# Score columns of two attention layers become rows on all partitions: by DMA through a DRAM scratch row instead of by transposes on TensorE

## The chip, the cores and the metric

The kernel runs on one core of one Trainium2 chip. The metric is the device time of one execution in microseconds (us); the time before is the median of three runs. The profile is one further execution, taken by the hardware profiler. Its engines are PE (TensorE, matmuls), PEld (TensorE weight loads, which overlap PE), DVE (VectorE), ACT (ScalarE), POOL (GpSimd) and SP (SyncE, which in this kernel only issues DMAs).

## The reference

Input is a batch of 64 graphs with 256 nodes and 256 features each (`x`, 64 x 256 x 256, float32), and an adjacency matrix per graph (`adj`, 64 x 256 x 256, int32). Four layers follow, each with a layer norm and a relu in front and a residual around it:

- layer 0: masked self attention with 8 heads
- layer 1: graph attention with one head
- layer 2: three rounds of messages `A^T (h W)` into a GRU cell
- layer 3: graph attention with 4 heads

What the change concerns are the scores of layers 1 and 3, cut to their core:

```python
# layer 1
f1 = Wh @ a1; f2 = Wh @ a2
e = leaky_relu(f1[:, :, None] + f2[:, None, :], 0.2)
attention = softmax(where(mask > 0, e, -9e15), axis=1)
out = elu(attention @ Wh)
# layer 3, per head h
s_src = einsum('bnhc,hc->bnh', f, a_src); s_dst = einsum('bnhc,hc->bnh', f, a_dst)
logits = leaky_relu(s_src[:, :, None, :] + s_dst[:, None, :, :], 0.2)
probs = softmax(where(adj == 1, logits, -9e15), axis=2)
```

A score matrix is the sum of a column (one number per row node) and a row (one number per column node). On the chip nodes lie on partitions. The column is then one number per partition, which an activation adds as its bias for nothing. The row has to lie on every one of the 128 partitions, and this is what both kernels have to make from a column.

## The kernel before, in words

Two graphs are one "pair" (512 nodes, T = 4 tiles of 128 nodes), and there are 32 pairs. A short preparation loads and combines weights. After it the kernel describes every step of every pair as a task: an engine, an estimated duration, and the buffers that it reads and writes (`add`, line 59). `Plan.order` (line 96) then takes tasks greedily by their earliest start in its own model of time, over all pairs, and so writes one fixed order of instructions per engine. It does this for 18 settings (how many `w4` buffers stay spare for the oldest pair, and how finely start times are compared), and `Plan.best` (line 179) keeps the setting whose order comes out shortest in a model with jitter. Matmuls of layer 2 come last among PE tasks that can start at the same moment, so they fill PE while other layers wait for DVE and ACT. On the chip every engine runs its list in order; waits between engines and DMAs are semaphores. A DMA task counts as 0.7 us on SP plus a latency (3.5 us for an adjacency, 3.0 us for `x`).

Buffers are counted by `SLOTS` (line 237): 28 work buffers `w4` of 4 KB per partition, 2 `adj` of 4 KB, 8 banks of PSUM (`ps`), 4 `w2` of 2 KB, 4 of `x`, and small ones. A buffer is taken when its first task is ordered, and comes free after its last.

The steps around the change:

- `load_adj` (530) loads a pair's adjacency once per layer, after the layer norm's statistics. The mask tasks (551, 687, 971) turn it into additive bf16 masks; layer 2 (790) turns it into a float matrix `am` in a `w4` buffer of its own.
- Layer 1 (683): four products give `Wh` and the two score columns; line 701 copies the columns to `f12`. The task `spread` (707) turns each of four columns into a row on all partitions by a transpose of the column broadcast to 128 x 128 (`row_to_all`, line 679; the trace shows its line 681). The row lies in a PSUM bank `psf`. Four Prelu activations (716) read it with the other column as bias. Eight bf16 transposes bring the mask (728), and mask add, max, exp and the product (760) follow.
- Layer 3 (968): four products (978), copied by DVE with a bias (982) into `f`. For each of 4 heads `spread` (989) makes a row of 512 numbers by four transposes (line 681 too), and an eviction (line 444 on ACT or 445 on DVE) takes it to a `w4` buffer of `sd`. Then for each tile of 128 nodes come four Prelu (1006), mask add (1012), max (1017), four exp (542), eight transposes (1029) with evictions, and per graph a product (1050), transposes back (1065), a scaling (1072) and the residual (1077).

Of the kernel before, what the change touches and what calls it, by code (L numbers as in the profile page):

```python
# [11 lines left out]
FP = mybir.dt.float32  # L12
BF = mybir.dt.bfloat16
I32 = mybir.dt.int32
AF = mybir.ActivationFunctionType
ALU = mybir.AluOpType
AX = mybir.AxisListType

P = 128
# [19 lines left out]
class Plan:  # L39
# [19 lines left out]
    def add(self, forms, reads=(), writes=(), latency=0.0, claims=()):  # L59

        t = Task()
        t.pair, t.forms = len(self.pairs) - 1, [forms] if isinstance(forms, tuple) else forms
        t.before, t.after, t.bufs, t.latency = set(), [], [], latency
        t.end = t.engine = None
        t.order, t.layer = len(self.pairs[-1]), self.layer  # L70
        for items, writing in ((reads, False), (writes, True)):
            for item in items:
                buf, part = item if isinstance(item, tuple) else (item, None)
                if buf not in t.bufs:
                    t.bufs.append(buf)
                keys = [part] if part is not None else list(buf.parts) + [None]
                for key in keys:
                    last, readers = buf.parts.setdefault(key, [None, []])
                    whole = buf.parts.get(None, [None, []])
                    for x in (last, whole[0]):  # L80
                        if x is not None:
                            t.before.add(x)
                    if writing:
                        t.before.update(readers)
                        t.before.update(whole[1])
                for key in keys:
                    if writing:
                        buf.parts[key] = [t, []]
                    else:
                        buf.parts[key][1].append(t)  # L90
        t.before.discard(t)
        t.bufs += [b for b in claims if b not in t.bufs]
        self.pairs[-1].append(t)
        return t
# [101 lines left out]
def tile_adj_preln_d4(  # L196
# [33 lines left out]
    T = 4  # L230
# [5 lines left out]

    SLOTS = {
        "x": (4, [P, T * D], FP, 0),
        "adj": (2, [P, T * N], I32, 1),
        "w4": (28, [P, T * D], FP, 9),  # L240
        "f3": (2, [P, T, E3], FP, 0),
        "mask": (4, [P, T * N], BF, 1),
        "ps": (8, [P, 512], FP, 2),
# [5 lines left out]
        "zs": (6, [P, H0], FP, 2),  # L249
        "rz": (6, [P, H0], FP, 2),  # L250
        "f12": (2, [P, T, 2], FP, 0),
    }
    psum = ctx.enter_context(tc.tile_pool(name="psum", bufs=1, space=bass.MemoryType.PSUM))
    tiles = {"ps": [psum.tile([P, 512], FP, name=f"ps_{i}") for i in range(SLOTS["ps"][0])]}
# [151 lines left out]


    work = ctx.enter_context(tc.tile_pool(name="work", bufs=1))
    for tag, (n, shape, dtype, _) in SLOTS.items():
        if tag not in tiles:  # L410
            tiles[tag] = [work.tile(shape, dtype, name=f"{tag}_{i}") for i in range(n)]
    plan = Plan({tag: v[0] for tag, v in SLOTS.items()}, {tag: v[3] for tag, v in SLOTS.items()})

    def buf(tag):
        return Buf(tag, tiles[tag])

    def w4():
        return buf("w4")

    def bank():  # L420
        return buf("ps")
# [4 lines left out]
    def dve2(n):  # L426
        return 0.065 + n / 1920.0
# [7 lines left out]
    def tok(ap, d=D):  # L435
        return ap.rearrange("p (t d) -> p t d", d=d)
# [91 lines left out]
                mm(ps()[:, c * D : (c + 1) * D], chunk(src, k, 2 * g + c), rhs[:, k, :], start=k == 0, stop=k == 1)  # L528

    def load_adj(p, mv):  # L530
        at = buf("adj")
        add(
            (SP, 0.7, lambda: nc.sync.dma_start(tok(at(), N), adj[2 * p : 2 * p + 2].rearrange("g (c p) d -> p (g c) d", p=P))),
            reads=[mv], writes=[at], latency=3.5,
        )
        return at
# [11 lines left out]
    def layer0(xt, p):  # L548
        at, hT = norm_relu_T(xt, p)
        mb = buf("mask")  # L550
        add((V, dve2(T * N), lambda: nc.vector.tensor_scalar(mb(), at(), 0.0, MASKED, ALU.is_le, ALU.mult), True), reads=[at, hT], writes=[mb])
        for g in range(2):
            add(
                (G, pool(2 * D), lambda g=g: nc.gpsimd.tensor_add(
# [121 lines left out]
        half = lambda: xt()[:, g * N2 : (g + 1) * N2]  # L676
        add((V, dve(N2), lambda: nc.vector.tensor_add(half(), ps(), half())), reads=[ps], writes=[(xt, g)])

    def row_to_all(ps, col):

        nc.tensor.transpose(ps, col.to_broadcast([P, P]), ident)  # L681

    def layer1(xt, p):
        at, hT = norm_relu_T(xt, p)
        m1 = buf("mask")
        add(
            (V, dve2(T * N), lambda: nc.vector.tensor_scalar(
                m1(), at(), 0.0, MASKED, ALU.is_le, ALU.mult), True),
            reads=[at, hT], writes=[m1],
        )  # L690
        wh, f12 = w4(), buf("f12")
        for t in range(T):
# [9 lines left out]
                reads=[ps], writes=[(f12, t)],  # L702
            )
            add((A, act(D), lambda t=t, ps=ps: nc.scalar.copy(tok(wh())[:, t, :], ps()[:, 0:D])), reads=[ps], writes=[(wh, t)])
        psf = bank()

        def spread():
            for t in range(T):
                row_to_all(psf()[:, t * P : (t + 1) * P], f12()[:, t, 0:1])

        e = w4()
        add((PE, 4 * TURN, spread), reads=[f12], writes=[psf], claims=[e])
        for t in range(T):
            g = t // 2
            add(
                (A, act(N, 1), lambda t=t, g=g: nc.scalar.activation(
                    tok(e(), N)[:, t, :], psf()[:, g * N : (g + 1) * N], AF.Prelu,
                    bias=f12()[:, t, 1:2], alpha=ALPHA)),
                reads=[psf, f12], writes=[(e, t)],
            )  # L720
        psb = bank()
        psm = lambda: psb().bitcast(BF).rearrange("p (t n) -> p t n", n=N)
# [63 lines left out]

    def layer2(xt, p):
        at, hT, h = norm_relu_T(xt, p, tokens=True)
        am = w4()
        add((V, dve2(T * N), lambda: nc.vector.tensor_scalar(am(), at(), 0.0, None, ALU.not_equal), True), reads=[at, hT], writes=[am])  # L790
        at_o = lambda b, o: tok(b(), N2)[:, o, :]

        def messages(h):
# [174 lines left out]
    def layer3(xt, p):  # L968
        at, hT = norm_relu_T(xt, p)
        mb = buf("mask")  # L970
        add((V, dve2(T * N), lambda: nc.vector.tensor_scalar(mb(), at(), 1.0, MASKED, ALU.not_equal, ALU.mult), True), reads=[at, hT], writes=[mb])
        f = buf("f3")
        for t in range(T):
            ps = bank()
# [8 lines left out]
                reads=[ps], writes=[(f, t)],  # L983
            )
        sd = [w4() for i in range(2)]
        for h in range(H3):
            ps = bank()

            def spread(h=h, ps=ps):
                for t in range(T):  # L990
                    row_to_all(ps()[:, t * P : (t + 1) * P], f()[:, t, D + H3 + h : D + H3 + h + 1])

            add((PE, 4 * TURN, spread), reads=[f], writes=[ps], claims=[sd[h // 2]])
            add(
                evict(N2, lambda h=h: tok(sd[h // 2](), N2)[:, h % 2, :], ps),
                reads=[ps], writes=[(sd[h // 2], h % 2)],
            )
        for g in range(2):
            zs, rz = buf("zs"), buf("rz")
            eT = [w4() for k in range(2)]  # L1000
            for ti in range(2):
                t = 2 * g + ti
                e, mx = w4(), buf("mx")
                for h in range(H3):
                    add(
                        (A, act(N, 1), lambda t=t, g=g, h=h, e=e: nc.scalar.activation(
                            tok(e(), N)[:, h, :], tok(sd[h // 2](), N2)[:, h % 2, g * N : (g + 1) * N], AF.Prelu,
                            bias=f()[:, t, D + h : D + h + 1], alpha=ALPHA)),
                        reads=[(sd[h // 2], h % 2), (f, t)], writes=[(e, h)],
                    )  # L1010
                add(
                    (V, dve(T * N), lambda t=t, e=e: nc.vector.tensor_tensor(
                        tok(e(), N), tok(e(), N), tok(mb(), N)[:, t : t + 1, :].to_broadcast([P, H3, N]), ALU.add), True),
                    reads=[mb], writes=[e],
                )
                add(
                    (V, dve(T * N), lambda e=e, mx=mx: nc.vector.tensor_reduce(
                        mx()[:, 0:H3], tok(e(), N), AX.X, ALU.max, negate=True)),
                    reads=[e], writes=[mx],
                )  # L1020
                rows = [(i, i, H3 * ti + i) for i in range(H3)]
                add(exp_group(e, mx, zs, rows, f"3_{p}_{t}"), reads=[mx], writes=[e, (zs, ti)])
                for k in range(2):
                    ps = bank()

                    def turn(k=k, ps=ps, e=e):
                        for i in range(2):
                            for c in range(2):
                                nc.tensor.transpose(  # L1029
                                    tok(ps(), P)[:, 2 * i + c, :], tok(e(), N)[:, 2 * k + i, c * P : (c + 1) * P], ident  # L1030
                                )

                    add((PE, 4 * TURN, turn), reads=[e], writes=[ps], claims=[eT[k]])
                    add(
                        evict(
                            N2,
                            lambda dst=eT[k], ti=ti: tok(dst(), N)[:, :, ti * P : (ti + 1) * P],
                            lambda ps=ps: tok(ps(), P),
                        ),
                        reads=[ps], writes=[(eT[k], ti)],  # L1040
                    )
# [90 lines left out]
```

## Time and profile before

| | |
|---|---|
| median of three runs | 4248.58 us (4247.72 to 4248.71) |
| the profiled execution: its own time, its span | 4250.05 us, 4247.8 us |
| PE busy | 4178.7 us, 98% of the span |
| DVE, ACT, POOL busy | 3061.3 us (72%), 2521.8 us (59%), 603.1 us (14%) |
| DMA queue of SP | 7.9% of 16 engines' time |
| granted TensorE clock, mean | 0.996 |

"Busy" is time in which an instruction of the engine runs. PE's row counts matmuls, whose ends are modelled. A group line of the profile gives line, engine, operation, result and operands, shape and count; then the time that the group covers, the mean duration of one in ns, and the idle time of the engine just before it with what ended that.

### The profile page before, as it was taken

Reading aid. Unit: us, or ns where it says so; the run is one execution under the profiler, and the core shown is the slowest. Engines: PE = TensorE matmul, PEld = TensorE weight load, DVE = VectorE, ACT = ScalarE, POOL = GpSimd, SP = SyncE. Lnnn points to the kernel's source line nnn. Section 1 sums busy time; section 2 is a strip of 40 time slices with the busy share of each in tenths; the row PEclk is TensorE's granted clock in tenths of the full one; section 3 lists DMA queues with packets and bytes.
Section 4 is the critical chain, followed back from the end, with each engine's and each line's share of the span. In section 5 each row is a group of like instructions: output and inputs, shape, how many; then the busy total and the mean of one; then the engine's idle time right before and its main releaser. Section 6 shows DMA issues by size and latency. Waiting matters only on the chain.

```text
span 4247.8 us, 56704 instructions
## 1 busy us (share of the span) xinstructions
PE 4178.7 (98%) x20720; PEld 2674.7 (63%) x20720; DVE 3061.3 (72%) x5920; ACT 2521.8 (59%) x6744; POOL 603.1 (14%) x602
## 2 busy tenths in 40 slices
PE   7999999999999999999999999999999999999997
PEld 4666666666666666666666666666666666666654
DVE  5977767767777767776667776677786758767555
ACT  4856556656566646566556666565665656666444
POOL 1011111111111111111111111111111111111110
PEclk9999999999999999999999999999999999999998
DMA  3000000000000000000110000000000000001000
GB/s 92 26 6 31 31 30 16 23 23 31 30 30 16 16 30 31 31 30 1 30 30 31 29 27 6 30 30 31 16 23 23 31 30 28 28 6 35 15 10 15
DMA packets 110567, 109.29 MB, mean 26 GB/s; under 512 B 7376, under 2 KB 110032, under 8 KB 110288
## 3 DMA queue, kind: packets, MB, share of 16 engines
q1 hardware_dynamic: 110288, 105.67, 7.9%
q8 instruction: 163, 2.67, 0.3%
q14 instruction: 116, 0.95, 0.1%
HBM read 88.88 MB, written 16.78 MB: 25 GB/s over the span
## 4 chain that ended last, share of the span: by engine, by line
PE 92%; DVE 5%; ACT 2%; issue 0%; DMA 0%; SPq 0%; POOL 0%; POOLq 0%; DVEq 0%; ACTq 0%
PE ps L821 28%; PE ps L901 16%; PE ps L802 8%; PE ps L528 5%; PE ps L637 5%; PE ps L566 5%; PE ps L587 3%; PE ps L658 3%; PE ps L978 3%; PE ps L760 3%; PE ps L1050 3%; PE ps L505 2%; PE ps L1029 2%; PE ps L697 2%; PE ps L681 1%; PE ps L887 1%
## 5 line engine op out<-in xcount | busy, mean ns | idle before, releaser
L542 ACT ACTIVATE w<-w,mx 128x256 f32<-128x256 f32 x1664 | 824.0, 502 | 184.6 <-DVE mx L608 135.7
L444 ACT COPY w<-ps 128x512 f32<-128x512 f32 x1027 | 573.4, 585 | 529.6 <-PE ps L802 168.8
L821 PE MATMUL ps<-w,whhT 128*128 128x512 f32 x1536 | 724.5, 596 | 3.8 <-DVE w L445 3.8
L821 PE MATMUL ps<-w,giT 128*128 128x512 f32 x1536 | 714.1, 594 | 0.0
L821 PEld LDWEIGHTS ps<-w,giT 128*128 128x128 f32 x1536 | 288.2, 190 | 344.4 <-issue 331.9
L445 DVE COPY w<-ps 128x512 f32<-128x512 f32 x573 | 380.4, 685 | 159.2 <-PE ps L887 57.3
L821 PEld LDWEIGHTS ps<-w,whhT 128*128 128x128 f32 x1536 | 274.9, 191 | 247.6 <-issue 228.0
L901 PE MATMUL ps<-whhT,w 128*128 128x512 f32 (+1 forms) x1024 | 364.0, 492 | 0.0
L901 PE MATMUL ps<-giT,w 128*128 128x512 f32 (+1 forms) x1024 | 359.6, 488 | 0.0
L802 PE MATMUL ps<-w,w 128*128 128x256 f32 x1536 | 354.5, 381 | 0.0
L601 DVE SCALAR_TENSOR_TENSOR w<-ps,mask 128x512 f32<-128x512 f32 x512 | 333.9, 678 | 15.3 <-PE ps L587 15.1
L542 ACT ACTIVATION_READ_ACCUMULATOR w<-w,mx 128x1 f32 x1664 | 322.5, 194 | 0.0
L624 ACT ACTIVATE w<-w,rz 128x256 f32<-128x256 f32 x664 | 289.2, 502 | 50.8 <-DVE rz L615 50.7
L802 PEld LDWEIGHTS ps<-w,w 128*128 128x128 f32 x1536 | 286.5, 190 | 50.0 <-issue 11.8
L608 DVE TENSOR_REDUCE mx<-w 128x4 f32<-128x1024 f32 x256 | 309.6, 1209 | 1.7
L901 PEld LDWEIGHTS ps<-giT,w 128*128 128x128 f32 x1024 | 192.0, 190 | 152.5 <-issue 135.4
L637 PEld LDWEIGHTS ps<-ident,w 128*128 128x128 f32 x2048 | 234.8, 141 | 80.6 <-issue 47.6
L858 POOL TENSOR_TENSOR w<-w,w 128x512 f32<-128x512 f32 x128 | 165.5, 1294 | 800.4 <-ACT w L853 763.5
L637 PE MATMUL ps<-ident,w 128*128 128x128 f32 x2048 | 268.2, 274 | 3.9 <-DVE w L624 1.6
L901 PEld LDWEIGHTS ps<-whhT,w 128*128 128x128 f32 x1024 | 188.3, 192 | 106.9 <-issue 91.2
L955 POOL TENSOR_TENSOR w<-w,w 128x512 f32<-128x512 f32 x64 | 81.8, 1279 | 1127.4 <-ACT w L954 1127.4
L833 ACT ACTIVATE w<-ps,brz 128x512 f32<-128x512 f32 x128 | 87.6, 684 | 252.5 <-PE ps L821 252.3
(127 smaller groups left out, 6439.4 us busy)
## 6 DMA issues: line engine op xcount, KB each, us to landing
adj<-in_adj_dram SPq DMA_DIRECT2D x128, 512.0 KB, 4.0
x<-in_x_dram SPq DMA_DIRECT2D x64, 256.0 KB, 2.8
out_dram<-x SPq DMA_DIRECT2D x64, 256.0 KB, 2.2
gg_sb<-in_L_gnn_weight_dram SPq DMA_DIRECT2D x3, 256.0 KB, 5.7
wih_sb<-in_L_gnn_w_ih_dram SPq DMA_DIRECT2D x1, 768.0 KB, 7.7
whh_sb<-in_L_gnn_w_hh_dram SPq DMA_DIRECT2D x1, 768.0 KB, 9.2
wq_sb<-in_L_gnn_Wq_dram SPq DMA_DIRECT2D x1, 256.0 KB, 3.1
wk_sb<-in_L_gnn_Wk_dram SPq DMA_DIRECT2D x1, 256.0 KB, 3.2
```

Of the source, the lines that this page charges most:

```text
L444: (A, act(n), lambda: nc.scalar.copy(dst(), src())),
L445: (V, dve(n), lambda: nc.vector.tensor_copy(dst(), src())),
L528: mm(ps()[:, c * D : (c + 1) * D], chunk(src, k, 2 * g + c), rhs[:, k, :], start=k == 0, stop=k == 1)
L542: nc.scalar.activation(tok(e(), N)[:, i, :], tok(e(), N)[:, i, :], AF.Exp, bias=mx()[:, m : m + 1], accum_out=zs()[:, z : z + 1],)
L566: mm(ps(), w[:, k, o * P : (o + 1) * P], tok(hT(), N2)[:, k, :], start=k == 0, stop=k == 1)
L601: (V, dve(N2), lambda s=s, j=j, b=b, t=t: nc.vector.scalar_tensor_tensor(tok(s(), N)[:, 2 * j : 2 * j + 2, :], tok(b(), N), SCALE, tok(mb( ...
L608: (V, dve(4 * N), lambda s=s, mx=mx, h4=h4: nc.vector.tensor_reduce(mx()[:, h4], tok(s(), N), AX.X, ALU.max, negate=True)),
L624: op(tok(s(), N)[:, i, :], tok(s(), N)[:, i, :], rz()[:, z : z + 1])
L637: nc.tensor.transpose(tok(ps(), P)[:, 2 * i + c, :], tok(s(), N)[:, 2 * k + i, c * P : (c + 1) * P], ident,)
L802: mm(ps()[:, g * N : (g + 1) * N], tok(h())[:, t, o * P : (o + 1) * P], tok(am(), N)[:, t, :], start=c == 0, stop=c == 1,)
L821: mm(ps(), w[:, k, c0 : c0 + P], at_o(src, k), start=n == 0, stop=n == 2 * len(terms) - 1)
L901: mm(out, chunk(src, k, t), w[:, k, c0 : c0 + n], start=m == 0, stop=m == 2 * len(terms) - 1)
```

## The change

Rows of scores no longer come from TensorE. A new helper `to_all` writes the column to a scratch row in DRAM by one DMA, in which every number is a piece of its own, and reads the row back by one DMA (layer 1) or two (layer 3) whose source is repeated for each of 128 partitions. All three are SP tasks. In layer 1 the row lands in a `w2` buffer, from which the Prelu read it (before: from PSUM). In layer 3 a small DVE copy first gathers the four columns of `f` in a buffer `dst` (128 x 16); the row has 2048 numbers; and the two `sd` buffers now hold one graph each with all four heads, not two heads each with both graphs.

Adjacency loads have no buffers of their own any more: they take a `w4`, of which there are 30 in place of 28, and layer 2 makes `am` in place in the buffer in which the adjacency landed.

```diff
     SLOTS = {
-        "adj": (2, [P, T * N], I32, 1),
-        "w4": (28, [P, T * D], FP, 9),
+        "w4": (30, [P, T * D], FP, 9),
...
+        "dst": (4, [P, T, H3], FP, 0),
+        "row1": (4, [N2], FP, 0),
+        "row3": (4, [H3 * N2], FP, 0),
...
+    dram = ctx.enter_context(tc.tile_pool(name="dram", bufs=1, space=bass.MemoryType.DRAM))
...
     def load_adj(p, mv):
-        at = buf("adj")
+        at = w4()
         add(
-            (SP, 0.7, lambda: nc.sync.dma_start(tok(at(), N), adj[2 * p : 2 * p + 2].rearrange("g (c p) d -> p (g c) d", p=P))),
+            (SP, 0.7, lambda: nc.sync.dma_start(tok(at().bitcast(I32), N), adj[2 * p : 2 * p + 2].rearrange("g (c p) d -> p (g c) d", p=P))),
             reads=[mv], writes=[at], latency=3.5,
         )
...
-    def row_to_all(ps, col):
-
-        nc.tensor.transpose(ps, col.to_broadcast([P, P]), ident)
+    def to_all(row, src, columns, dsts):
+
+        add(
+            (SP, 0.7, lambda: nc.sync.dma_start(row().rearrange("(c p) -> p c", p=P).unsqueeze(2), columns())),
+            reads=[src], writes=[row], latency=3.0,
+        )
+        for i, dst in enumerate(dsts):
+
+            def spread(i=i, dst=dst):
+                n = dst().shape[1]
+                part = row()[i * n : (i + 1) * n]
+                nc.sync.dma_start(dst(), bass.AP(tensor=part.tensor, offset=part.offset, ap=[[0, P], [1, n]]))
+
+            add((SP, 0.7, spread), reads=[row], writes=[dst], latency=3.5)
...
     # layer 1
-        psf = bank()
-
-        def spread():
-            for t in range(T):
-                row_to_all(psf()[:, t * P : (t + 1) * P], f12()[:, t, 0:1])
-
+        f1 = buf("w2")
+        to_all(buf("row1"), f12, lambda: f12()[:, :, 0:1], [f1])
         e = w4()
-        add((PE, 4 * TURN, spread), reads=[f12], writes=[psf], claims=[e])
...
-                    tok(e(), N)[:, t, :], psf()[:, g * N : (g + 1) * N], AF.Prelu,
+                    tok(e(), N)[:, t, :], f1()[:, g * N : (g + 1) * N], AF.Prelu,
...
     # layer 2
-        am = w4()
-        add((V, dve2(T * N), lambda: nc.vector.tensor_scalar(am(), at(), 0.0, None, ALU.not_equal), True), reads=[at, hT], writes=[am])
+        am = at
+        add(
+            (V, dve2(T * N), lambda: nc.vector.tensor_scalar(am(), am().bitcast(I32), 0.0, None, ALU.not_equal), True),
+            reads=[hT], writes=[am],
+        )
...
     # layer 3
-        for h in range(H3):
-            ps = bank()
-
-            def spread(h=h, ps=ps):
-                for t in range(T):
-                    row_to_all(ps()[:, t * P : (t + 1) * P], f()[:, t, D + H3 + h : D + H3 + h + 1])
-
-            add((PE, 4 * TURN, spread), reads=[f], writes=[ps], claims=[sd[h // 2]])
-            add(
-                evict(N2, lambda h=h: tok(sd[h // 2](), N2)[:, h % 2, :], ps),
-                reads=[ps], writes=[(sd[h // 2], h % 2)],
-            )
+        dst = buf("dst")
+        add(
+            (V, 0.09, lambda: nc.vector.tensor_copy(dst(), f()[:, :, D + H3 : E3]), True), reads=[f], writes=[dst]
+        )
+        to_all(buf("row3"), dst, lambda: dst().rearrange("p t h -> p (t h)").unsqueeze(2), sd)
...
-                            tok(e(), N)[:, h, :], tok(sd[h // 2](), N2)[:, h % 2, g * N : (g + 1) * N], AF.Prelu,
+                            tok(e(), N)[:, h, :].rearrange("p (c n) -> p c n", n=P),
+                            sd[g]().rearrange("p (c h n) -> p h c n", h=H3, n=P)[:, h], AF.Prelu,
                             bias=f()[:, t, D + h : D + h + 1], alpha=ALPHA)),
-                        reads=[(sd[h // 2], h % 2), (f, t)], writes=[(e, h)],
+                        reads=[sd[g], (f, t)], writes=[(e, h)],
```

The masks of layers 0, 1 and 3 read the adjacency through the same bitcast. Nothing else changes in the code, but the order of every engine's instructions is written anew by `Plan` from the changed tasks.

More of the change, by code (lines that the diff above doesn't have):

```diff
@@ L408, in tile_adj_preln_d4 @@
     work = ctx.enter_context(tc.tile_pool(name="work", bufs=1))
+    dram = ctx.enter_context(tc.tile_pool(name="dram", bufs=1, space=bass.MemoryType.DRAM))
     for tag, (n, shape, dtype, _) in SLOTS.items():
         if tag not in tiles:
-            tiles[tag] = [work.tile(shape, dtype, name=f"{tag}_{i}") for i in range(n)]
+            tiles[tag] = [(dram if tag in ("row1", "row3") else work).tile(shape, dtype, name=f"{tag}_{i}") for i in range(n)]
     plan = Plan({tag: v[0] for tag, v in SLOTS.items()}, {tag: v[3] for tag, v in SLOTS.items()})
@@ L550, in layer0 @@
         mb = buf("mask")
-        add((V, dve2(T * N), lambda: nc.vector.tensor_scalar(mb(), at(), 0.0, MASKED, ALU.is_le, ALU.mult), True), reads=[at, hT], writes=[mb])
+        add((V, dve2(T * N), lambda: nc.vector.tensor_scalar(mb(), at().bitcast(I32), 0.0, MASKED, ALU.is_le, ALU.mult), True), reads=[at, hT], writes=[mb])
         for g in range(2):
@@ L687, in layer1 @@
             (V, dve2(T * N), lambda: nc.vector.tensor_scalar(
-                m1(), at(), 0.0, MASKED, ALU.is_le, ALU.mult), True),
+                m1(), at().bitcast(I32), 0.0, MASKED, ALU.is_le, ALU.mult), True),
             reads=[at, hT], writes=[m1],
@@ L716, in layer1 @@
                 (A, act(N, 1), lambda t=t, g=g: nc.scalar.activation(
-                    tok(e(), N)[:, t, :], psf()[:, g * N : (g + 1) * N], AF.Prelu,
+                    tok(e(), N)[:, t, :], f1()[:, g * N : (g + 1) * N], AF.Prelu,
                     bias=f12()[:, t, 1:2], alpha=ALPHA)),
-                reads=[psf, f12], writes=[(e, t)],
+                reads=[f1, f12], writes=[(e, t)],
             )
@@ L970, in layer3 @@
         mb = buf("mask")
-        add((V, dve2(T * N), lambda: nc.vector.tensor_scalar(mb(), at(), 1.0, MASKED, ALU.not_equal, ALU.mult), True), reads=[at, hT], writes=[mb])
+        add((V, dve2(T * N), lambda: nc.vector.tensor_scalar(mb(), at().bitcast(I32), 1.0, MASKED, ALU.not_equal, ALU.mult), True), reads=[at, hT], writes=[mb])
         f = buf("f3")
```

## The prediction

> **What bounds the kernel now.** I read the first part of the page, then the busy time by stretches (fill, middle, drain).
>
> ```profile
> PE 4178.7 (98%) x20720; PEld 2674.7 (63%) x20720; DVE 3061.3 (72%) x5920; ACT 2521.8 (59%) x6744; POOL 603.1 (14%) x602
> ```
>
> ```profile
> 200.00:4150.00 3950.00, 3936.74 (x19388) 2515.77 (x19387) 2866.05 (x5513) 2356.56 (x6275) 570.44 (x562) 1.00 0.08 24
> 4150.00:4247.80 97.80, 71.78 (x306) 43.80 (x304) 50.12 (x76) 39.59 (x107) 9.14 (x8) 0.87 0.05 17
> ```
>
> The first fence is the page's busy times, the second the stretches; there the columns are the stretch, its length, then busy us of PE, PEld, DVE, ACT and POOL. From 200 to 4150 us PE is busy for 3936.74 of 3950 us, 99.7%, at full clock; DVE has 73%. Only preparation (0 to 65) and drain show real gaps. So in the middle a microsecond of matmul removed is a microsecond gained, and a microsecond in which PE finds nothing ready is one lost. Next, the groups of the line that goes:
>
> ```profile
> L681 PE MATMUL ps<-ident,f 128*128 128x128 f32 x640 | 80.8, 273 | 0.2 <-DVE f L982 0.2
> L681 PEld LDWEIGHTS ps<-ident,f 128*128 128x128 f32 x640 | 72.0, 137 | 16.8 <-issue 14.2 <-DVE mv L464 1.7 <-DVE f L982 0.4
> ```
>
> A matmul shows 273 ns, but neighbours overlap. What a group costs is in the chain that ended last (start, us, what), around 2027 and 2110 us:
>
> ```profile
> 2027.44 0.44 PE ps L681 x4
> 2027.88 10.30 PE ps L821 x24
> ...
> 2066.13 0.45 PE ps L728 x8
> ...
> 2110.82 1.89 PE ps L681 x16
> ```
>
> Layer 1's four take 0.44 us, layer 3's sixteen 1.89 us. Layer 1's mask transposes (L728) come 38 us after its rows in this pair: its mask is late (L687 at 2063.50 in DVE's timeline) and PE fills the time with other pairs' matmuls. Latency of a pair is not what binds; work on PE is.
>
> Last, the DMAs (KB each, median us from issue to landing):
>
> ```profile
> adj<-in_adj_dram SPq DMA_DIRECT2D x128, 512.0 KB, 4.0
> x<-in_x_dram SPq DMA_DIRECT2D x64, 256.0 KB, 2.8
> out_dram<-x SPq DMA_DIRECT2D x64, 256.0 KB, 2.2
> ...
> bih_sb<-in_L_gnn_b_ih_dram SPq DMA_DIRECT2D x1, 3.0 KB, 5.3
> b_sb<-in_L_gnn_b_dram SPq DMA_DIRECT2D x1, 1.0 KB, 2.3
> ```
>
> The last two fetch numbers of 4 bytes one by one (768 and 256), the nearest thing to the new column writes; the first of them queued behind weight loads.
>
> **What the Trainium skill says.** "DMA: Bandwidth & Descriptors", section "Two DMAs through the same engine are not ordered": a DMA that reads what an earlier one wrote must wait for that one's completion semaphore. So the two legs of `to_all` add up, and SP stands still between them. The same page, "Rules for kernel authors": a last dimension that isn't contiguous becomes one descriptor per element. The trace agrees: its packet records show four-byte packets for `bih_sb`. Its "Anatomy of one DMA" puts most of a fixed cost of about 2 us into the write receipt, HBM being heaviest. Here the smallest load lands in 2.3 us, but the 256 KB store to DRAM in 2.2, sooner than the load of that size (2.8), so I charge no extra for a DRAM target. "TensorE: Matmul & The Clock Gate", "Architectural detail: the array is 16× 32×32, not 1× 128×128": ACT and DVE queues are strict first in, first out. A late Prelu therefore holds up every eviction behind it.
>
> **The change part by part.**
>
> 1. *Transposes removed.* 0.44 + 1.89 = 2.33 us a pair, times 32 = 74.6 us of PE. (The group's 80.8 us counts overlap with neighbours; that is the upper end.)
>
> 2. *Evictions removed.* 4 per pair, 128 in all, at 585 ns (ACT) or 685 (DVE): 75 to 88 us over two engines. Both have room in the middle, so I count nothing; in the drain it is a gain of about 1 us. Added on DVE is one small copy, some 160 ns as line 701 takes: 5 us, under PE's cover. Without that cover it would lie in layer 3's chain at 0.16 us a pair.
>
> 3. *Prelu.* Layer 1's read SBUF instead of PSUM: 503 ns (L1006) against 483 (L716), 128 x 20 ns = 2.6 us of ACT, hidden. Layer 3's read in a strided order, for which no row stands; between 0 and the whole PSUM difference again, hidden too.
>
> 4. *Row write, layer 1.* 512 numbers on 16 engines are 32 each. From the packet records, `bih_sb` and `bhh_sb` moved 1592 four-byte packets between 7.5 and 9.5 us: 2.0 x 16 / 1592 = 20 ns each on an engine. 2.2 + 32 x 0.020 = 2.8 us. Read back, 256 KB: 2.8 us as `x`. From column to Prelu, with about 0.5 us for three hand-overs, 6.1 us. The order is written for 0.15 + 0.7 + 3.0 + 0.1 + 0.7 + 3.5 + 0.1 = 8.25 us, so data come before their place in ACT's list: no stall.
>
> 5. *Row write, layer 3.* 2048 numbers are 128 per engine: 2.2 + 128 x 0.020 = 4.8 us. A write may be dearer than a read. The lower end is 2.8 us, were short packets nearly free; for the upper I charge each as much as a packet of 1 KB, 46 ns in the median of the records: 2.2 + 5.9 = 8.1 us. I take 4.8, since they are the same four-byte pieces. Read back, 512 KB as an adjacency: 4.0 us; the second half, 0.5 us behind, is wanted later. With the copy (0.16) and hand-overs (0.5) it is 9.5 us. The order is written for 0.1 + 0.09 + 0.15 + 0.7 + 3.0 + 0.1 + 0.7 + 3.5 + 0.1 = 8.4. So the first Prelu is late by 1.1 us, and behind it on ACT the evictions of other pairs. How much PE then waits is set by slack. In the DVE timeline one mask add (L1012) starts at 2649.05, and the transposes that need its exp (L1029) at 2654.29: 5.2 us, for work of 1.21 + 1.22 + 2.07 (four exp) and hand-overs of about 0.4, 4.9 in all. Slack there is 0.3 us; in other pairs up to 2. With 0.8, PE loses 0.3 us a pair: 31 x 0.3 = 10 us. At both ends: none at 2.8; at 8.1 (late by 4.4, less 0.8) 31 x 3.6 = 110 us.
>
> 6. *SP.* Five DMAs a pair are added to eight, and SP waits between write and read for 3 to 5 us, with adjacency loads and `x` behind it. SP now waits up to 112 us at a time for an output to be ready, so it has room; a load that stands behind a row is late by at most that landing, and masks have waited 30 us and more without PE noticing. I count 0, at worst 2 us a pair (64 us). DMA engines go from 8% to some 12% busy; a row write that falls into an adjacency's transfer waits up to 2 us, in about one case of ten: 0.2 us x 32 = 6 us at most, inside the slack.
>
> 7. *Adjacency in `w4`.* A load holds a `w4` for about 10 us in four layers, 40 us per 130 us a pair takes, 0.3 buffer on average; layer 2 saves its second one for a moment, and there are two more. I count 0. A gain isn't excluded (masks 30 us late vanish), but PE has nothing left to gain from it; a loss would need the pool to run dry.
>
> 8. *Drain.* The last pair's layer 3 is exposed: its bias copy ends at 4221.37 and the first Prelu starts at 4222.44, 1.1 us later. With 9.5 us that is +8.4, less 1 for the evictions: +7.4 us.
>
> Sum: 4247.8 - 74.6 + 10 + 7.4 = 4190.6 us of span. The profiled execution took 4250.05, 2.25 us around its span, and the median of runs is 0.8 over that span: 4191.4, so **4191 us**, 1.3% less.
>
> **The rivals.**
>
> *No stall at all* (4.8 or less for the row write, more slack): 4190.6 - 10 + 0.8, 4181 us. For it: PE's 99.7%, its waits for exp before L1029 of only 25.9 us in the whole run. Against: that the margins are small.
>
> *Slower: the row write of layer 3 lands late.* Place: SP's wait between write and read, then ACT's first L1006. At 8.1 us, 4181 + 110 = 4291. The gain left after the drain, 67 us, is used up at 67 / 31 = 2.2 us of stall a pair, so at a landing of 3.7 + 0.8 + 2.2 = 6.7 us, or 35 ns per number (the order itself allows 8.4 - 0.16 - 0.5 - 4.0 = 3.7 us, slack 0.8). For it: no store of four bytes is in the trace. Against: fetches take 20 ns.
>
> *Nothing gained: SP becomes the queue that everything waits in.* Adjacency loads stand behind row waits and PE stalls for masks by 2 us a pair: 4181 + 64 = 4245. Against: SP's long idle waits.
>
> That transposes would not go is excluded by the code: PE must show 20080 matmuls.
>
> **How the numbers follow.** About 0.2% (8.5 us) is what a measurement of this kernel tells from no change. The forecast has a chance of 0.45, no stall 0.20, the late row 0.22, SP's queue 0.08, and 0.05 a new order that leaves PE holes of its own. Faster: 0.45 + 0.20, and a third of the SP case, 0.67; within 0.2%: 0.06; slower: 0.27. The likeliest case's own range is 4180 to 4225. Down to 4168 takes in 80.8 us saved and no stall or drain; up to 4295 takes in the upper price of the row write, beyond which lie some 0.12.
>
> **What would show it.** PE busy down by some 75 us, no line 681 of before, and between 200 us and the drain still 99% or more busy: steps 1, 2 and 7. The row write of layer 3 landing in 4 to 6 us and its reads in about 4: step 5; above 6.7 with ACT idle before layer 3's Prelu, the slower rival. Layer 1's Prelu without idle time before it: step 4. Some 9 us from the last pair's bias copy to its first Prelu: step 8. What would make me wrong is a price of four-byte stores that I couldn't see, or an order whose margins are tighter than those shown.

## The result, and the profile after

The changed kernel takes 4622.36 us in the median of four runs (4615.11 to 4630.08), the kernel before 4248.17: 1.088 times as long, with a 95% interval of 1.086 to 1.090. I had forecast 4191 and a range up to 4295. The profiled execution took 4626.73 us, with a span of 4624.9, 377.1 us more than before.

First the page of the changed kernel: busy us and share of the span, then the chain that ended last.

```profile
PE 4251.7 (92%) x20080; PEld 2666.3 (58%) x20080; DVE 3045.1 (66%) x5911; ACT 2478.6 (54%) x6637; POOL 635.2 (14%) x622
...
PE 63%; DMA 19%; DVE 10%; ACT 6%; issue 1%; SPq 0%; POOL 0%; POOLq 0%; DVEq 0%; ACTq 0%
PE ps L833 16%; PE ps L913 12%; DMA row<-dst 8%; DMA w<-row 6%; DMA row<-f 5%; PE ps L814 5%; PE ps L569 4%; PE ps L531 4%; PE ps L640 4%; PE ps L1056 3%; ACT w L1011 3%; PE ps L769 3%; PE ps L1035 2%; PE ps L508 2%; PE ps L661 2%; PE ps L711 2%
```

640 matmuls are gone (20720 to 20080), as the change says. But the chain that had no DMA now has 19% of it, and its three DMA lines are the new rows. PE was idle for 4624.9 - 4251.7 = 373 us, before for 69: 304 us more. PE's busy time is 73 us longer although 81 us of transposes went, so the matmuls that stayed took 154 us more. 304 + 154 - 81 = 377, the whole difference. Most of the 154 us is the clock, whose mean granted share fell from 0.996 to 0.959. The clock's records show what is behind these means: half clock for 380 us in 61 stretches (before: 36 us in 5), in which PE was busy for 276 us (before: 19). If a matmul takes twice as long there, as those below do, this makes (276 - 19) / 2 = 128 us, an estimate. The other 26 us stay unexplained.

Busy time by stretches shows that the loss is not mainly one of fill or drain (columns: stretch, length, PE, PEld, DVE, ACT, POOL, clock, DMA share, GB/s):

```profile
1000.00:2000.00 1000.00, 933.49 (x4472) 586.21 (x4472) 689.10 (x1334) 559.99 (x1512) 140.85 (x137) 0.97 0.12 32
4500.00:4625.00 125.00, 80.86 (x319) 47.66 (x317) 57.98 (x84) 44.12 (x122) 11.65 (x10) 0.83 0.10 30
```

In the same stretch of the kernel before PE was busy for 996.86 of 1000 us. The DMA view (KB each, median us from issue to landing) shows what is late:

```profile
w<-in_adj_dram SPq DMA_DIRECT2D x128, 512.0 KB, 5.5
w<-row SPq DMA_DIRECT2D x64, 512.0 KB, 4.7
x<-in_x_dram SPq DMA_DIRECT2D x64, 256.0 KB, 2.8
...
w<-row SPq DMA_DIRECT2D x32, 256.0 KB, 4.9
...
row<-f SPq DMA_DIRECT2D x32, 2.0 KB, 10.3
row<-dst SPq DMA_DIRECT2D x32, 8.0 KB, 11.1
```

A row write of 2 KB takes 10.3 us and one of 8 KB 11.1. The order was written for 3.7. An adjacency, 4.0 us before, takes 5.5; a later run with quick rows in the same order has 5.5 too, so the slow row writes are not the reason for that. One late row in the chain (start, us, what):

```profile
2037.57 0.09 DVE dst L1000
...
2037.68 11.45 DMA row<-dst
...
2049.27 4.21 DMA w<-row
...
2053.50 2.90 ACT w L1011 x7
2056.40 0.47 ACT w L447
```

From the copy to the first Prelu (now line 1011) it is 16 us. Behind the Prelu in ACT's list stands an eviction (L447) for which PE waits, as PE's timeline of that moment shows in brackets:

```profile
2051.60 1.02 PE L833 MATMUL ps<-w,giT 128*128 128x512 f32 x2
2056.92 2.07 PE L833 MATMUL ps<-w,giT 128*128 128x512 f32 x2 [4.29 <-ACT w L447]
```

These are matmuls of layer 2, of another pair: the late row stops work that has nothing to do with it. Two of them take 1.02 us before the wait and 2.07 after it. The stretches of that moment (last three columns: clock, DMA share, GB/s) show why:

```profile
2052.60:2056.70 4.10, 0.03 (x1) 0.00 (x0) 1.43 (x2) 3.20 (x8) 0.00 (x0) 1.00 0.38 127
2056.70:2060.10 3.40, 3.18 (x8) 1.52 (x8) 3.37 (x3) 3.40 (x13) 0.00 (x0) 0.50 0.00 0
```

After 4.1 us almost without a matmul PE runs at half clock for 3.4 us. So a stall costs twice, as idle time and as slower matmuls behind it. Before each of the 61 stretches at half clock, PE was idle for at least 1.6 of the last 6.8 us. The waits of the whole run (total us, times, longest):

```profile
ACT w L1011 <- DMA w<-row: 266.5, 35, 21.3
DVE w L1018 <- ACT w L1011: 230.6, 42, 16.9
ACT w L725 <- DMA w<-row: 197.9, 28, 8.5
```

### The profile page after: what moved, and what is told of

Read it like the earlier page. It is cut to its first block, busy times and chain, and to the rows that moved or that the text cites. A ratio compares the mean times of both kernels' runs of the same rounds, so it can differ in the third digit from the quotient of the medians.

```text
span 4624.9 us, 56016 instructions
## 1 busy us (share of the span) xinstructions
PE 4251.7 (92%) x20080; PEld 2666.3 (58%) x20080; DVE 3045.1 (66%) x5911; ACT 2478.6 (54%) x6637; POOL 635.2 (14%) x622
## 4 chain that ended last, share of the span: by engine, by line
PE 63%; DMA 19%; DVE 10%; ACT 6%; issue 1%; SPq 0%; POOL 0%; POOLq 0%; DVEq 0%; ACTq 0%
PE ps L833 16%; PE ps L913 12%; DMA row<-dst 8%; DMA w<-row 6%; DMA row<-f 5%; PE ps L814 5%; PE ps L569 4%; PE ps L531 4%; PE ps L640 4%; PE ps L1056 3%; ACT w L1011 3%; PE ps L769 3%; PE ps L1035 2%; PE ps L508 2%; PE ps L661 2%; PE ps L711 2%
## 5 line engine op out<-in xcount | busy, mean ns | idle before, releaser
L447 ACT COPY w<-ps 128x512 f32<-128x512 f32 x972 | 540.1, 584 | 603.1 <-PE ps L814 163.2
L833 PE MATMUL ps<-w,whhT 128*128 128x512 f32 x1536 | 747.8, 615 | 55.9 <-ACT w L447 38.2
L833 PE MATMUL ps<-w,giT 128*128 128x512 f32 x1536 | 742.2, 610 | 58.5 <-ACT w L447 35.3
L448 DVE COPY w<-ps 128x512 f32<-128x512 f32 x500 | 332.0, 684 | 166.1 <-PE ps L531 52.6
L814 PE MATMUL ps<-w,w 128*128 128x256 f32 x1536 | 373.6, 395 | 26.5 <-ACT w L447 25.8
L1011 ACT ACTIVATE w<-w,f 128x256 f32<-128x256 f32 x512 | 214.8, 497 | 266.5 <-DMA w<-row 266.5
L1018 DVE TENSOR_TENSOR w<-w,mask 128x1024 f32<-128x1024 f32 x128 | 154.6, 1222 | 230.7 <-ACT w L1011 230.6
L870 POOL TENSOR_TENSOR w<-w,w 128x512 f32<-128x512 f32 x128 | 165.9, 1296 | 849.5 <-ACT w L865 849.5
L627 ACT ACTIVATE w<-w,rz 128x256 f32<-128x256 f32 x620 | 271.6, 502 | 18.1 <-DVE rz L618 17.5
L475 POOL TENSOR_SCALAR rs<-mv 128x4 f32<-128x4 f32 x128 | 33.7, 263 | 1611.8 <-DVE mv L467 1563.6
```

The lines of the kernel that those rows point to most:

```text
L447: (A, act(n), lambda: nc.scalar.copy(dst(), src())),
L448: (V, dve(n), lambda: nc.vector.tensor_copy(dst(), src())),
L627: op(tok(s(), N)[:, i, :], tok(s(), N)[:, i, :], rz()[:, z : z + 1])
L814: mm(ps()[:, g * N : (g + 1) * N], tok(h())[:, t, o * P : (o + 1) * P], tok(am(), N)[:, t, :], start=c == 0, stop=c == 1,)
L833: mm(ps(), w[:, k, c0 : c0 + P], at_o(src, k), start=n == 0, stop=n == 2 * len(terms) - 1)
```

## Experiments

My first theory after the result (A): the orders of the engines are written for rows that land in 3.7 us, and every wait comes from that. The rivals: a longer way from column to Prelu starves PE even in a fitting order (B); the shared buffer pool does the harm (C); the new work itself takes back the gain (D). Later ones are named where they arise. All times are medians of runs beside runs of the kernel before on the same chip (4248.0 to 4248.6).

**The parts one by one.** Adjacency in `w4` alone, on the kernel before:

```diff
-        "adj": (2, [P, T * N], I32, 1),
-        "w4": (28, [P, T * D], FP, 9),
+        "w4": (30, [P, T * D], FP, 9),
...
-        at = buf("adj")
+        at = w4()
...
-        am = w4()
+        am = at
```

> The kernel before with one part of the change: adjacency from the w4 pool of 30, am in place; rows by transposes as before. Theory A: nothing, 4235 to 4265 us. Rival C, the shared pool is what makes loads late: 4350 us or more.

Measured: 4258.64 us, ratio 1.0024 (1.0014 to 1.0034). Ten us lost; C falls as the main cause.

Layer 1's row alone by DMA (layer 3 as before the change), and layer 3's alone:

```diff
 # layer 1 by transposes again (layer 3 alone by DMA); the other run does the same for layer 3
-        to_all(buf("row1"), f12, lambda: f12()[:, :, 0:1], [f1])
...
+        add((PE, 4 * TURN, spread), reads=[f12], writes=[psf], claims=[e])
```

> The changed kernel with layer 3's rows by transposes and evictions again; layer 1's row stays with the DMAs. Theory A: each late row costs on its own, layer 1 by some 198/464 of the whole: 4330 to 4450 us. Rival B': layer 1 is harmless because its mask is later than its row: 4220 to 4260.

> The changed kernel with layer 1's row by transposes again; layer 3's rows stay with the DMAs. Theory A: 4400 to 4520 us. Rival B': nearly all of the loss, 4580 to 4640.

Measured: 4399.88 us with layer 1's row (ratio 1.0356, 1.0341 to 1.0372) and 4468.58 with layer 3's (1.0518, 1.0503 to 1.0534). The losses are 151 and 220 us. Both contain the adjacency's 10; counted once, they add up to 361 of the whole 374. So each late row costs on its own. B' falls: that some masks are later than layer 1's row doesn't protect it.

**An order that knows the landings.** Same instructions, other numbers for the plan:

```diff
-            reads=[src], writes=[row], latency=3.0,
+            reads=[src], writes=[row], latency=lands,   # 10.0 in layer 1, 10.8 in layer 3
...
-            add((SP, 0.7, spread), reads=[row], writes=[dst], latency=3.5)
+            add((SP, 0.7, spread), reads=[row], writes=[dst], latency=4.5)
```

> The changed kernel, but the order is written for the landings that the trace of it showed: 10.0 and 10.8 us of latency for the row writes of layers 1 and 3 (before 3.0), 4.5 for the reads (before 3.5). Theory A, the order is written for data 7 us too early, and ACT, then PE, stand at the Prelu: 4190 to 4240 us, ACT idle before L1011 and L725 under 60 us in all (464 in the changed kernel), granted clock back at 0.99. Rival B, the longer way of a pair itself, or SP waiting between write and read, starves PE: over 4400 us.

Measured: 4305.66 us, ratio 1.0135 (1.0120 to 1.0150). ACT's idle time before the Prelu fell from 464 us to 28. An order that knows the landings is 317 us faster, so most of the loss comes from the wrong numbers. But the forecast for A was 4190 to 4240 with the clock at 0.99 (measured 0.982), and the gain didn't come. In the trace the loads of `x` now landed in 4.6 us in the median (2.8 before) and DVE waited 113 us for them. The next run tells the plan of that too:

```diff
-            writes=[(xt, g)], latency=3.0,
+            writes=[(xt, g)], latency=5.0,
...
-            reads=[mv], writes=[at], latency=3.5,
+            reads=[mv], writes=[at], latency=5.0,
```

> As the run whose order was written for rows landing in 10 us, with adjacencies and x written for 5.0 us of latency too (3.5 and 3.0 before), since they landed late behind the rows (5.4 and 4.6 us). Theory A: the wait of DVE for x (113 us) goes, 4200 to 4260 us. Rival D: 4290 or more.

Measured: 4256.17 us (1.0019, 1.0011 to 1.0026). Better by 49, at the upper end of A's range, and still no gain; DVE still waits 50 us for `x`.

**What makes the row write slow.** A program with nothing but DMAs, in which each row write is finished before the row is read back:

```diff
+        nc.sync.dma_start(ra.rearrange("(c p) -> p c", p=P).unsqueeze(2), src[:, 0:4].unsqueeze(2))   # wacol: 4 B x 512
...
+        nc.sync.dma_start(rd.rearrange("(p c) -> p c", p=P), src[:, 0:4])                             # wdrow: 16 B x 128
...
+        nc.sync.dma_start(rf.rearrange("(p c s) -> p c s", c=4, s=128)[:, :, 0:1], src[:, 0:4].unsqueeze(2))   # wfapart: 4 B x 512, 512 B from one to the next
```

> None of the layers is computed: x is copied to the output, and between, one after the other and each six times, stand writes of SBUF to DRAM in pieces of 4 B (128, 512 or 2048 of them, neighbours in DRAM coming from different partitions; 512 also each on a 512-byte block of its own), 16, 32, 64, 512 and 2048 B (128 of each), and one piece of 2 KB; each is read back before the next. Twice a load of 256 KB is issued right behind a write, once of 4-byte pieces and once of 512-byte pieces. Theory A1, the landing is set by the piece: 4-byte writes land in 8 to 10 us whatever their number, 512 B and more in about 2.2, those between in between, and the load behind the 4-byte write lands late too (over 6 us) but not behind 512-byte pieces (about 3). Theory A2, by the count: 128 pieces of 4 B land in under 4 us, like 128 of 64 B. Theory A3, by the same block of DRAM being written from many engines: 4 B each on its own block land in under 4 us.

The DMA view of that program (KB each, median us to landing; `wbcol` is 2048 pieces of 4 B, `wccol` 128, `wjrow` 128 of 32 B, `werow` 128 of 64 B, `whrow` 128 of 2 KB):

```profile
whrow<-src SPq DMA_DIRECT2D x6, 256.0 KB, 2.0
...
wacol<-src SPq DMA_DIRECT2D x6, 2.0 KB, 8.8
...
wbcol<-src SPq DMA_DIRECT2D x6, 8.0 KB, 11.6
...
wccol<-src SPq DMA_DIRECT2D x6, 0.5 KB, 7.7
...
wdrow<-src SPq DMA_DIRECT2D x6, 2.0 KB, 2.3
...
wjrow<-src SPq DMA_DIRECT2D x6, 4.0 KB, 1.4
...
werow<-src SPq DMA_DIRECT2D x6, 8.0 KB, 1.4
...
wfapart<-src SPq DMA_DIRECT2D x6, 2.0 KB, 2.1
```

For each of these writes the trace has the landing of only one of the six. The others follow from SP's timeline, since the read of a row is issued when its write has landed. After the first repetition, which still overlaps the copying of `x`, they agree within 0.6 us, with one exception: the 16-byte pieces land in 1.4 us four times, and the 2.3 in the view is their one slow case.

The three rows of neighbouring 4-byte pieces land in 7.7, 8.8 and 11.6 us for 128, 512 and 2048 pieces. So it isn't the count (A2 falls): sixteen times the pieces cost 4 us more. Nor is it the size by itself (A1 falls): the 512 pieces of 4 B that lie 512 B apart land in 2.1 us. It takes both, short pieces and neighbours, as A3 forecast. That many engines writing one block is the reason, as A3 has it, is not shown: 16-byte pieces side by side, from different partitions, are quick. In the records of the changed kernel the packets of such a write are done 1.3 us (512 numbers) or 2.2 us (2048) after its issue; the other 9 us pass before the completion is seen. Why it is seen so late, no run here shows. Pieces of 16 B side by side (1.4 us) are already as quick as pieces of 2 KB (2.0). The loads meant to stand behind a write were issued elsewhere in that program, so this part of the question moved to a later run.

**The same order with quick rows.** If the landing is the cause, changing only the layout of the scratch row must bring most of it back. A partition's numbers lie side by side, and the Prelu read them with a step of 16 or 32 B; the plan's numbers, and with them the order, stay those of the changed kernel:

```diff
-            (SP, 0.7, lambda: nc.sync.dma_start(row().rearrange("(c p) -> p c", p=P).unsqueeze(2), columns())),
+            (SP, 0.7, lambda: nc.sync.dma_start(to(row()), columns())),
+            # layer 1: "(p c) -> p c", 16 B; layer 3: "(g p c) -> p g c", 32 B
...
-                    tok(e(), N)[:, t, :], f1()[:, g * N : (g + 1) * N], AF.Prelu,
+                    tok(e(), N)[:, t, :].rearrange("q (c p) -> q c p", p=P),
+                    f1().rearrange("q (p c) -> q c p", p=P)[:, 2 * g : 2 * g + 2, :], AF.Prelu,
```

> The changed kernel, its order written for the same latencies (3.0), but the row is laid out with a partition's numbers side by side: 128 pieces of 16 B in layer 1, 256 of 32 B in layer 3, and the Prelu read it back in a strided order. If pieces of this size land in 4 us or less: 4180 to 4240 us. If the landing stays at 9 to 11 us: 4580 to 4650.

Measured: 4302.79 us, ratio 1.0127 (1.0110 to 1.0144). The rows, and what the strided reads cost ACT (columns as in the page's groups):

```profile
row<-f SPq DMA_DIRECT2D x32, 2.0 KB, 1.4
row<-dst SPq DMA_DIRECT2D x32, 8.0 KB, 1.5
```

```profile
L1012 ACT ACTIVATE w<-w,f 128x256 f32<-128x256 f32 x512 | 344.5, 757 | 12.5 <-DMA w<-row 12.5
...
L725 ACT ACTIVATE w<-w,f 128x256 f32<-128x256 f32 x128 | 87.6, 757 | 0.9 <-DMA w<-row 0.7
```

320 us came back in an unchanged order (in the two traces every engine's list is the same, instruction for instruction), although each Prelu grew from 497 to 757 ns. So the layout of the row write is shown to cause most of the loss, by the late rows and by what the write holds up behind it (below) together. Neither of my two numbers was met: the landing is 1.4 us, yet the time isn't 4180 to 4240. The Trainium skill, "SBUF — State Buffer", section "Door 1: The DMA port swizzle", says that reads that step beyond a 16-byte line pay for each new line; the 260 ns over 256 elements agree with that in kind.

**Orders written for the quick rows.** The numbers of two runs are shown in short, side by side; the third run has the true times and the adjacency buffers of the kernel before.

```diff
-            reads=[src], writes=[row], latency=3.0,      # true times | with slack
+            reads=[src], writes=[row], latency=0.8,      # 0.8        | 10.0
+            ... spread latency=4.2                       # 4.2        | 4.5
+            ... adjacency latency=5.0                    # 5.0        | 5.0
+            ... Prelu act(N, 1) + 0.26                   # both
```

> Rows in pieces of 16 and 32 B, and the order written for what those runs showed: latency 0.8 for the row write, 4.2 for its reads, 5.0 for adjacencies (3.5 before), 0.26 us more for each Prelu with strided reads. Theory A, what is left of the loss (54 us) is orders written for the wrong times: 4180 to 4220 us. Rival D, the work that the rows bring itself (166 us more of ACT, reads in the DMA queue before adjacencies) takes PE's gain: 4260 to 4310.

> As the run with pieces and an order written for them, with the adjacency's two buffers and 28 w4 as before the change. The adjacency part alone cost 10 us on the kernel before; if that adds up, 10 us less than its twin, else the same within 10.

> Rows in pieces that land in 1.5 us, in an order written as if they took 10.0 (and 4.5 for the reads, 5.0 for adjacencies): all data come far ahead of their place. Theory A: no wait for rows at all, within 20 us of the run whose order is written for the true times. Rival B, a longer way from column to Prelu costs PE by itself: 40 us or more above it.

Measured: true times 4212.62 us (0.9918, 0.9903 to 0.9933); the same with adjacency buffers of its own 4196.38 (0.9880, 0.9865 to 0.9895); with slack 4173.16 (0.9824, 0.9807 to 0.9840). All three beat both kernels. B falls: an order that lets 10 us pass for rows that land in 2.3 and 1.5 us in that run is the fastest of all, 39 us ahead of the one with true times. A had forecast a difference within 20 us, so it doesn't explain this one. D falls as well. The adjacency's own buffers make 16 us, where 10 was forecast if the parts add up. The fastest run's page and its middle:

```profile
PE 4103.4 (98%) x20080; PEld 2605.6 (62%) x20080; DVE 2988.4 (72%) x5928; ACT 2630.3 (63%) x6629; POOL 630.5 (15%) x613
```

```profile
1000.00:2000.00 1000.00, 999.05 (x4897) 631.52 (x4896) 731.10 (x1450) 650.35 (x1641) 156.80 (x151) 1.00 0.11 35
```

PE is busy for 999 of 1000 us again, and PE's total is 75.3 us below the kernel before (4178.7): what the transposes were worth.

**Controls.** Is that gain the adjacency's margin, which this order has too? The kernel before with `latency=5.0` for adjacencies:

> The kernel before, rows by transposes, with adjacencies written for 5.0 us in place of 3.5: a control for the fastest run, which has this margin too. Theory A, the gain there is the transposes' 75 us: 4240 to 4260 us. Rival F, the gain is the margin for adjacencies: 4170 to 4210.

Measured: 4257.24 us (1.0022, 1.0014 to 1.0030). No; F falls. And would the 4-byte rows do as well in an order with wide margins (rows 18 us, reads 6.5, adjacencies and `x` 7.0)?

> The changed kernel with its rows in 4-byte pieces that land in 10 to 11 us, in an order written with wide margins: 18 us for the row write, 6.5 for its reads, 7.0 for adjacencies and x. Theory A, the late landing hurts only where the order doesn't know of it: 4170 to 4210 us. Rival E, the pieces hurt by themselves, through other loads that land late behind them: 4250 or more.

Measured: 4254.61 us (1.0017, 1.0008 to 1.0026). No: A alone isn't enough, and E's forecast, 4250 or more, came true. In this run's DMA view the loads of `x` and the adjacencies are late (medians of the 19 and 32 landings that the trace has):

```profile
w<-in_adj_dram SPq DMA_DIRECT2D x128, 512.0 KB, 7.4
...
x<-in_x_dram SPq DMA_DIRECT2D x64, 256.0 KB, 11.3
```

One case by stretches (last three columns: clock, DMA share, GB/s). A row write of 512 pieces is issued at 2055.85, two `x` loads and an adjacency right behind it:

```profile
2055.80:2057.80 2.00, 2.00 (x14) 1.84 (x13) 0.71 (x2) 0.86 (x2) 0.00 (x0) 1.00 0.44 93
2057.80:2066.30 8.50, 8.50 (x34) 6.16 (x34) 1.38 (x2) 1.17 (x2) 0.00 (x0) 1.00 0.84 42
2066.30:2069.30 3.00, 3.00 (x9) 1.32 (x8) 1.72 (x8) 0.00 (x0) 0.00 (x0) 1.00 0.76 228
```

For 8.5 us the DMA engines count as busy for 84% but move 42 GB/s; then the loads go at 228.

The changed kernel and its twin with quick rows, which have one order and a landing for every load, show the same thing. In both, the same five loads of `x` and five adjacencies are issued while a row write is unfinished. In the changed kernel they land in 11.0 to 12.4 and 12.5 to 14.3 us; with quick rows in 4.3 to 4.7 and 4.9 to 6.4. Two last runs separate this further. A program that issues a 256 KB load right behind a row write, order fixed:

> None of the layers is computed: x is copied to the output. Between, in a fixed order and six times, a write of a row to DRAM with a load of 256 KB issued right behind it, then both finished before the next pair: rows in neighbouring 4-byte pieces (512 and 2048 of them), in 16-byte pieces (128), and in 4-byte pieces on a block of 512 B each (512). Theory E, an unfinished write of neighbouring 4-byte pieces holds up the engines' later transfers: the load lands in 9 us or more behind 512 and 2048 such pieces, and in about 3 behind the two others. Rival G, loads in the kernels were late for another reason: about 3 us behind all four.

```profile
behindkcol<-in_x_dram SPq DMA_DIRECT2D x6, 256.0 KB, 11.6
...
behindlrow<-in_x_dram SPq DMA_DIRECT2D x6, 256.0 KB, 4.1
...
behindfapart<-in_x_dram SPq DMA_DIRECT2D x6, 256.0 KB, 3.3
...
behindbcol<-in_x_dram SPq DMA_DIRECT2D x6, 256.0 KB, 11.8
```

Behind neighbouring 4-byte pieces the load lands in 11.6 and 11.8 us; behind 16-byte pieces in 4.1, behind 4-byte pieces that lie apart in 3.3. The unfinished write holds up what is issued behind it on the same queue: it lands itself after 9.5 and 11.2 us here, and the load follows soon after. So this part of E is shown, and G falls. The twin of the wide-margin run with 16- and 32-byte pieces:

> The twin of the run with 4-byte pieces and wide margins (18, 6.5, 7.0 and 7.0 us): the same margins, rows in pieces of 16 and 32 B. Theory E, the pieces alone made the difference between 4255 and 4173: 4170 to 4200 us. Rival H, the wide margins did: 4235 or more.

Measured: 4224.33 us (0.9943, 0.9927 to 0.9960), between the two forecasts. With equal margins the run with quick rows is 30 us faster, and the other 51 us to the fastest run lie in the order. The 30 us aren't the pieces' alone either: the Prelu's price in the plan differs (0.26 us), so the twins' orders do too. The four orders with quick rows and rewritten numbers spread from 4173 to 4224 us; what makes one of them better is not settled.

## Why the prediction was wrong, by its own steps

*What bounds the kernel* and *step 1* (74.6 us of PE): right. The fastest of the four orders with quick rows has this gain, 75 us, and keeps PE at 99.9% in the middle. The other three gain 24 to 52 us.

*Step 5, the landing of layer 3's row*: the step that failed. I priced the write by its pieces, 2.2 + 128 x 0.020 = 4.8 us, upper end 8.1. The pieces themselves are no slower than I priced them (2048 are done 2.2 us after the issue), but the landing is 11.1 us, because neighbouring 4-byte pieces in DRAM complete some 9 us after their last packet. The rows I took the price from fetched 4-byte numbers from DRAM; the only store in the trace had pieces of 1 KB. And on the strength of that store I charged nothing for what the Trainium skill says of write receipts in "DMA: Bandwidth & Descriptors", section "Anatomy of one DMA". That section is about DMAs issued from GpSimd, and no run here shows that the 9 us are a receipt. The slower rival was the right mechanism at the right place, with its deciding point at 6.7 us; its price was taken too low, and with it its chance.

*Step 4, layer 1's row*: failed on the same term, and worse, since I let it scale with the count: 2.8 us forecast, 10.3 measured, so "no stall" became 198 us of idle ACT and 151 us of loss for layer 1 alone.

*The sum of stalls*: with the measured landings in place my working gives for layer 3 a Prelu late by 0.16 + 0.5 + 11.1 + 4.7 - 8.4 = 8.1 us, less 0.8 of slack 7.3, times 31 = 226 us. For layer 1 it gives 0.5 + 10.3 + 4.9 - 8.25 - 0.8 = 6.7, times 31 = 206. In the runs with one layer's rows alone PE's idle time grew from 69 us to 240 (layer 3) and to 181 (layer 1), by 171 and 112, drain and adjacency included. So the sum overstates the idle time. The whole losses, 220 + 60 of saved transposes - 13 of drain - 10 of adjacency = 257 us and 151 + 14 - 10 = 155, are 412 us together, near the sum's 432. That is luck: too much idle time stands in for the slower clock, which the sum lacks. The Trainium skill says in "TensorE: Matmul & The Clock Gate", section "Part 1: The HAM clock gate (the "warmup" mystery)", that idle PE falls to half clock; the trace agrees, with a clock of 0.50 after 4.1 us almost without a matmul.

*Step 6, SP*: I counted 0 and took a load behind a row to be late by at most its landing. Size and place are right (8 to 9 us late), but in the changed kernel only ten loads stand there. DVE's wait for `x` is 80 us in it and 32 with quick rows in the same order; what of the 320 us this makes is not separated. The forecast of DMA engines busy for some 12% came true (12.0%).

*Step 7, adjacency*: 0 forecast, 10 us measured on the kernel before. This may be no more than another order, since a latency changed alone moved the time by 9 us in the control. *Steps 2 and 3*: the copy (174 ns in the median, 160 forecast) and the Prelu (497 ns from SBUF, 503 forecast) cost what was said. *Step 8, drain*: 8.4 us forecast, 15.4 - 1.1 = 14.3 measured (last bias copy ends at 4585.23, first Prelu starts at 4600.60), by the same landing.

## What to carry to other kernels

Price a DMA by the layout of its destination, not by bytes and pieces: if no row of the profile stores pieces that small next to each other, bound the store from above with more than the dearest packet seen, or measure it alone. Where a fixed order is computed from assumed latencies, a latency told too short stops every engine that stands behind the waiting instruction. One told too long can cost little: 10 us for rows that land in about 2 gave the fastest order here, though 18 us, with wider margins for the loads too, gave one 51 us slower. And an operation off the bound engine can be worth exactly what the bound engine lost, but only once the replacement's data come before their place in line.

## What the runs showed of the hardware

- Writes to DRAM in neighbouring 4-byte pieces land in 7.7 us (128), 8.8 (512) and 11.6 (2048); 512 pieces of 4 B on blocks of 512 B in 2.1; 128 pieces of 16, 32 and 64 B side by side in 1.4 (16 B once in 2.3). Whether it is slow because several DMA engines write one block or because of the short pieces as such, and where between 4 and 512 B of distance it ends, was not measured.
- A load of 256 KB issued behind such a write on SP's queue is held up until the write completes: 11.6 to 11.8 us in place of 3.3 to 4.1. Other queues were not tried.
- After 4.1 us almost without a matmul PE's granted clock was 0.50 for 3.4 us, and two matmuls took 2.07 us in place of 1.02.
- A Prelu of 128 x 256 that reads SBUF in steps of 16 or 32 B takes 757 ns, with adjacent elements 497.
- A read of 256 KB that repeats one row of 2 KB for all partitions took 4.3 us, once 3.3 (a row written in one piece), a plain one of the same size 2.5.
